# ScalarE in program order during the three attention sweeps of a pre-norm block

## The chip, the cores and the metric

The kernel runs on one core of a Trainium2 chip. A core has five engines that run side by side and wait for one another by semaphores: TensorE (PE in the profile, its weight loads PEld), VectorE (DVE), ScalarE (ACT), GpSimd (POOL) and SyncE (SP, which here only issues transfers). Each engine takes its instructions one after the other from its own list. The metric is the device time of one execution in microseconds; the time of the kernel before is the median of three runs.

## The reference

One transformer block with 2048 tokens of width 1024, in float32:

```
x = x + attn(layernorm(x))
x = x + ffn(layernorm(x))

attn: q, k, v = h @ w.T + b, each as 32 heads of 32
      scores[s] = q[s] k[s]^T / sqrt(32)       # 32 x 32, heads against heads, per token
      context[s] = softmax(scores[s]) v[s]
ffn:  dq(w) = NF4 quantise and dequantise, blocks of 64 with their own absolute maximum
      (silu(h dq(w1)^T) * (h dq(w2)^T)) dq(w3)^T        # width 2752
```

Attention is between the heads of one token, so it never mixes tokens. The weights of the feed-forward come unquantised: quantising and dequantising 2752 x 1024 numbers three times is part of the work.

## The kernel before

**Three sweeps.** Attention goes over the tokens three times: sweep 1 computes q for all of them, sweep 2 computes k, the scores and the softmax, sweep 3 computes v, the context, the residual and the second layernorm. A sweep has 8 pairs (`for p in range(NP)`), a pair being 256 tokens. In the trace sweep 1 runs from 13 us to 244 us, sweep 2 to 498 us, sweep 3 to 776 us; what follows is the feed-forward.

**One pair.** `products` multiplies by a scheme of seven products instead of eight; each is 8 matmuls on PE (3.43 us, L326). Four of them add up in one bank `z` (three in sweep 1, where the sixth product has a bank `y` of its own), two in a bank `q`, one stands in `r`. The partial sums are needed between the products, so ACT copies them out: `g0` after the first product, `s7` from `q` after the second, `u2` after the third, `u4` after the fifth, and (in sweeps 2 and 3) `ce` after the sixth. As `z` goes on adding, PE may not start the third product (`T2`) before `g0` is copied, the fifth (`T1`) not before `u2`, the sixth (`B22`) not before `u4`. Between the products stands a call `fill(n)` with n = 7, 6, 2, 5, 3, 4 in this order, where other work is put:

- sweep 1, `fill(5)`: 16 transposes of the next pair's tokens on PE (L458), each group of four copied out twice by ACT (L461, L462); three PSUM buffers.
- sweep 2, `fill(7)`, `(2)`, `(5)`, `(4)`: half of the small score matmuls of one tile each (`part`, L406). After a second half comes the softmax: DVE takes the maximum (L562) and subtracts (L564), ACT takes the exponential (`pr`, L570), DVE sums, divides and transposes.
- sweep 3: context matmuls instead (L420), after a second half the residual and a layernorm on DVE; in `fill(5)` and `fill(3)` transposes (`keep_T`, L680) that ACT copies (L681).

**The background.** A generator (`background`) quantises the feed-forward weights, one [128, 1024] block (a job) at a time, and `advance(n)` takes n steps of it. A job has 17 steps. Twelve of them are one ACT instruction (`sg`, L229) and one DVE instruction that takes it in (`r`, L230); three are DVE alone; one is the next job's `absmax`: a DVE maximum, two small DVE instructions and 16 ACT multiplies (L182, `wn`); the last is 16 ACT multiplies of the result (L182, `r`), the scale step. `sg` has two buffers, `r` has two, so an `sg` waits for the DVE instruction two before it. Sweep 1 takes 7 steps in each pair (six fills without the fifth, and two at the pair's end), sweep 2 takes 8, sweep 3 takes 9. When the scale step is through, `flush` issues the job's transposes on PE (`ptw`, L156), half a job at a time, with an ACT copy each (`wop`, L157): in sweep 1 ahead of the steps of `fill(7)` and `fill(3)` and after the pair's products, in sweep 2 after the steps of `fill(5)` and `fill(3)` and after the pair's products, in sweep 3 after those of `fill(7)` and `fill(4)` and after the products.

**Who sets the order.** PE executes in the order of the program from the first sweep on (`manual_schedule`, L270). The order on ACT, DVE and the queues is set at build time by the scheduler: it plays the program through and, whenever an engine is free, gives it that ready instruction which stands first in the program. So an instruction of the background that is ready may be put ahead of a copy that still waits. What the scheduler has put into ACT's list stays there: the rows of ACT in the trace follow one another in exactly that order.

Of the kernel before, what the change touches and what calls it, by code (L numbers as in the profile page):

```python
# [68 lines left out]
def preln_block_kernel(  # L69
# [14 lines left out]
    nc = tc.nc  # L84
# [182 lines left out]
    pair = left.enter_context(tc.tile_pool(name="pair", bufs=1, side="left"))  # L267
    ps_pj = left.enter_context(tc.tile_pool(name="ps_pj", bufs=1, space=PSUM, side="left"))
    small = right.enter_context(tc.tile_pool(name="small", bufs=2, side="right"))
    ctx.enter_context(tc.manual_schedule(engines={nc.tensor.engine}))  # L270

    NP = NT // 2
    SA11, SA12, SA22, S1, S2, S3, S4 = range(7)
# [425 lines left out]
    for p in range(NP):  # L699
# [36 lines left out]
        advance(2)  # L736
        A = nextA
    hook["scale"] = "DVE"
    left.close()


# [317 lines left out]
```

## Time and profile before

| what | value |
|---|---|
| time, median of 3 runs | 2529.96 us (2529.02 to 2530.29) |
| the profiled execution | 2526.8 us, its span 2525.0 us |
| mean granted TensorE clock in it | 0.991 |
| busy, share of the span | PE 97%, DVE 76%, ACT 62%, POOL 4% |
| sweep 1, 13 to 244.4 us | PE 215.23, DVE 221.47, ACT 129.31 us busy of 231.4 |
| sweep 2, 244.4 to 498.2 us | PE 248.56, DVE 212.42, ACT 120.52 us busy of 253.8 |
| sweep 3, 498.2 to 776.2 us | PE 260.55, DVE 240.60, ACT 129.36 us busy of 278.0 |

A row of the timeline has the start in us, how long the piece lasts, the engine, the line of the kernel, the operation, what it writes `<-` what it reads, the shape and the number of instructions merged into the piece; brackets hold the idle time of the engine ahead of it and who ended that. A row of the waits has the engine, the line and what waited `<-` the engine, the line and the operand that released it, then the total in us, how often, and the longest.

### The profile page before, as it was taken

To read this page: it belongs to the slowest core of one execution; us is meant where nothing else is said; L and a number is where in the kernel's file an instruction comes from. 1 tells how busy PE (TensorE), PEld (TensorE's weight loads), DVE (VectorE), ACT (ScalarE), POOL (GpSimd) and SP (SyncE) were. 2 spreads that over 40 slices of the span, in tenths; PEclk is the share of its full clock that TensorE was granted. 3 is DMA by queue.
4 is the path that set the end of the run, shared out by engine and by line. 5 is a ranking of instruction groups with operands and counts; after the bars stand their busy time and mean duration, and the time that the engine had idled before them with its cause. 6 is when DMAs were issued, how large, how long until landed. Compare 5 with 4: busy or idle time off the path is not lost.

```text
span 2525.0 us, 36235 instructions
## 1 busy us (share of the span) xinstructions
PE 2445.7 (97%) x14160; PEld 1146.6 (45%) x14160; DVE 1923.1 (76%) x2088; ACT 1564.9 (62%) x3147; POOL 104.9 (4%) x152
## 2 busy tenths in 40 slices
PE   8999999999998999999999999999999999999998
PEld 4444455544444444444444444444444444444433
DVE  8999788878898578978789788887878878851022
ACT  3556544344543478878788787888877888851100
POOL 1010000000000000010000100001000010000100
PEclk9999999999999999999999999999999999999999
DMA  8779633656678574453743547436375353641574
GB/s 306 298 287 358 234 142 129 240 193 214 222 231 298 171 229 113 146 142 134 241 121 136 135 145 238 129 112 159 126 227 151 116 146 126 226 133 63 109 287 141
DMA packets 145323, 464.04 MB, mean 184 GB/s; under 512 B 12352, under 2 KB 66624, under 8 KB 125312
## 3 DMA queue, kind: packets, MB, share of 16 engines
q1 hardware_dynamic: 133056, 419.73, 45.9%
q0 software_dynamic: 11520, 41.95, 9.9%
q8 instruction: 111, 1.82, 0.3%
q14 instruction: 60, 0.49, 0.1%
q10 hardware_dynamic: 576, 0.05, 0.0%
HBM read 275.82 MB, written 185.86 MB: 183 GB/s over the span
## 4 chain that ended last, share of the span: by engine, by line
DVE 29%; PE 25%; ACT 11%; issue 4%; DMA 1%; DVEq 0%; ACTq 0%
DVE r L230 21%; PE po L951 12%; PE z L326 7%; ACT wn L182 4%; ACT r L182 3%; PE q L326 3%; ACT sg L229 2%; DVE r L223 2%; DVE r L225 2%; PE rr L326 1%; DVE am L194 1%; DVE r L241 1%; ACT wop L157 1%; PE po L963 1%; PE ptw L156 0%
## 5 line engine op out<-in xcount | busy, mean ns | idle before, releaser
L229 ACT ACTIVATE sg<-wn 128x1024 f32<-128x1024 f32 x780 | 814.3, 1051 | 358.1 <-DVE r L230 351.5
L230 DVE SCALAR_TENSOR_TENSOR r<-sg,r 128x1024 f32<-128x1024 f32 x780 | 946.9, 1214 | 68.5 <-ACT sg L229 26.2
L951 PE MATMUL po<-w,h 128*128 128x512 f32 x1344 | 594.0, 596 | 6.6 <-ACT acc L975 3.2
L951 PEld LDWEIGHTS po<-w,h 128*128 128x128 f32 x1344 | 250.0, 190 | 324.2 <-issue 288.3
L326 PE MATMUL z<-xB,w 128*128 128x512 f32 x720 | 325.4, 600 | 3.5 <-ACT u L889 1.8
L326 PE MATMUL z<-xT,w 128*128 128x512 f32 x656 | 296.3, 594 | 5.2 <-ACT u L882 5.0
L326 PE MATMUL q<-xT,w 128*128 128x512 f32 x656 | 290.9, 592 | 0.0
L182 ACT ACTIVATE wn<-wn,rc 128x64 f32<-128x64 f32 x1032 | 262.2, 336 | 45.1 <-DVE rc L202 45.1
L326 PEld LDWEIGHTS z<-xB,w 128*128 128x128 f32 x720 | 134.6, 192 | 166.9 <-issue 151.7
L326 PEld LDWEIGHTS q<-xT,w 128*128 128x128 f32 x656 | 123.6, 190 | 151.4 <-issue 149.2
L326 PEld LDWEIGHTS z<-xT,w 128*128 128x128 f32 x656 | 121.9, 190 | 153.9 <-issue 138.2
L326 PE MATMUL q<-wT,A 128*128 128x512 f32 x384 | 174.5, 598 | 2.3 <-DVE A L385 2.3
L326 PE MATMUL z<-wT,A 128*128 128x512 f32 x384 | 175.5, 600 | 1.1 <-ACT u L345 0.8
L326 PE MATMUL z<-wB,A 128*128 128x512 f32 x320 | 152.0, 619 | 13.4 <-ACT u L345 13.4
L182 ACT ACTIVATE r<-r,am 128x64 f32<-128x64 f32 x608 | 153.8, 339 | 14.7 <-DVE r L230 14.7
L326 PE MATMUL rr<-xB,w 128*128 128x512 f32 x328 | 147.5, 592 | 0.0
L975 ACT COPY acc<-po 128x512 f32<-128x512 f32 x160 | 91.3, 571 | 73.0 <-PE po L951 71.3
L194 DVE TENSOR_REDUCE am<-wn 128x16 f32<-128x1024 f32 (+1 forms) x65 | 78.4, 1206 | 76.1 <-ACT r L182 70.0
L981 POOL DMA_DIRECT2D x1d<-acc x80 | 70.2, 877 | 1497.3 <-ACT acc L975 1497.3
L326 PEld LDWEIGHTS q<-wT,A 128*128 128x128 f32 x384 | 72.6, 192 | 90.4 <-issue 84.8
L326 PEld LDWEIGHTS z<-wT,A 128*128 128x128 f32 x384 | 70.3, 190 | 79.8 <-issue 76.7
L885 DVE TENSOR_TENSOR g<-g,rr 128x512 f32<-128x512 f32 x41 | 28.0, 682 | 102.4 <-PE rr L326 102.4
(112 smaller groups left out, 2100.5 us busy)
## 6 DMA issues: line engine op xcount, KB each, us to landing
w<-wd SPq DMA_DIRECT2D x41, 1280.0 KB, 6.9
wd<-wop SPq DMA_DIRECT2D x21, 2048.0 KB, 6.7
x1d<-acc POOLq DMA_DIRECT2D x80, 512.0 KB, 5.1
wn<-in_w_dram SPq DMA_DIRECT2D x63, 512.0 KB, 3.9
w<-wd SPq DMA_DIRECT2D x62, 512.0 KB, 4.1
xT<-xdT SPq DMA_DIRECT2D x28, 1024.0 KB, 7.7
xB<-xdB SPq DMA_DIRECT2D x24, 1024.0 KB, 5.5
opD<-A SPq DMA_DIRECT2D x8, 1792.0 KB, 5.9
```

The lines of the kernel that those rows point to most:

```text
L157: nc.scalar.copy(o[:q, first + half], pt[:q])
L182: nc.scalar.mul(dst[:, ts(n, BLOCK)], src[:, ts(n, BLOCK)], by[:, n : n + 1])
L194: nc.vector.tensor_reduce(am[:, :nb], v.rearrange("p (b e) -> p b e", e=BLOCK), AX.X, ALU.max, apply_absolute_value=True,)
L223: nc.vector.scalar_tensor_tensor(r, v, edge, r, ALU.is_lt, ALU.max)
L225: nc.vector.scalar_tensor_tensor(r, v, edge, r, ALU.is_gt, ALU.subtract)
L229: nc.scalar.activation(t, v, AF.Copy, bias=-edge * by, scale=by)
L230: nc.vector.scalar_tensor_tensor(r, t, code, r, ALU.min, ALU.max)
L326: nc.tensor.matmul(dst, w[:, k, :], xop[:, k, :], start=start and k == 0, stop=stop and k == 3, skip_group_check=True,)
L885: nc.vector.tensor_tensor(self.g0, self.g0, r, ALU.add)
L951: nc.tensor.matmul(po, hs[c][j][:, ts(q, P)], w3T[c][:, ts(n, 512)], start=(c == g[0]), stop=(c == g[-1]), skip_group_check=True,)
L975: nc.scalar.copy(a[:, ts(n, 512)], po)
L981: nc.gpsimd.dma_start(x1d[i], a, accum_op=ALU.add)
```

## The change

During the three sweeps ACT is put under `manual_schedule` too, beside PE: it gets its instructions in the order in which the program issues them. After the last pair of sweep 3 that context is closed and the one for PE alone opened again, so from the feed-forward on the scheduler orders ACT as before. No instruction is added, taken away or changed, and the text of the program keeps its order.

```diff
-    ctx.enter_context(tc.manual_schedule(engines={nc.tensor.engine}))
+    by_hand = ExitStack()
+    by_hand.enter_context(
+        tc.manual_schedule(engines={nc.tensor.engine, nc.scalar.engine})
+    )
...
         advance(2)
         A = nextA
     hook["scale"] = "DVE"
+    by_hand.close()
+    ctx.enter_context(tc.manual_schedule(engines={nc.tensor.engine}))
     left.close()
```

## The prediction

> **What bounds the kernel now.** I read the page first: PE is busy 97% of the span, so time is gained or lost where PE waits. The change touches the sweeps alone, so I asked for PE's waits between 13 and 776.2 us (columns: who `<-` whom, us in total, times, longest):
>
> ```profile
> PE z L326 <- ACT u L345: 14.2, 6, 4.3
> PE pt L458 <- ACT V L462: 12.5, 4, 4.3
> ...
> PE pt L458 <- ACT AV L462: 1.0, 3, 0.3
> ```
>
> 27.7 us of PE's idle time end on an ACT copy. That is all that a better order on ACT can give, with what the clock adds. Next the timelines of PE and of ACT at the longest wait of sweep 3:
>
> ```profile
> 618.62 1.09 PE L680 MATMUL pt<-ident,x 128*128 128x128 f32 x8
> 624.02 5.40 PE L326 MATMUL z<-wB,A 128*128 128x512 f32 x8 [4.30 <-ACT u L345]
> ```
>
> ```profile
> 619.78 1.06 ACT L229 ACTIVATE sg<-wn 128x1024 f32<-128x1024 f32 x1 [6.05 <-DVE r L230]
> 621.11 1.06 ACT L229 ACTIVATE sg<-wn 128x1024 f32<-128x1024 f32 x1 [0.27 <-DVE r L230]
> 622.43 1.06 ACT L229 ACTIVATE sg<-wn 128x1024 f32<-128x1024 f32 x1 [0.27 <-DVE r L230]
> 623.40 0.57 ACT L345 COPY u<-z 128x512 f32<-128x512 f32 x1
> ```
>
> The product before ended at 617.4. The copy `u4` of it, at 623.40, stands behind three `sg` that come later in the program and run in step with DVE. PE idles 4.30 us, and its next eight matmuls take 5.40 us where 3.70 is usual: the granted clock is halved for 3.4 us. Such slow pieces follow the five long waits (4.04, 4.31, 4.30, 3.31, 3.69) with 1.1, 2.2, 1.7, 1.5 and 2.8 us above 3.70, together 9.3.
>
> The other side: the background runs far ahead of its place. Count its steps (7 a pair in sweep 1, 8 in sweep 2; scale steps are numbers 17, 34, 51, 68, 85, ... from 0). Number 68 belongs to sweep 2, pair 1, `fill(3)`; its PE transposes follow at once. The 16 multiplies and those transposes (ACT, then PE):
>
> ```profile
> 245.79 2.98 ACT L182 ACTIVATE r<-r,am 128x64 f32<-128x64 f32 x12 [0.57 <-DVE r L230]
> 248.67 0.56 ACT L345 COPY g<-z 128x512 f32<-128x512 f32 x1
> 249.14 1.06 ACT L182 ACTIVATE r<-r,am 128x64 f32<-128x64 f32 x4
> ```
>
> ```profile
> 293.64 3.70 PE L326 MATMUL z<-wB,A 128*128 128x512 f32 x8
> 297.18 0.60 PE L156 MATMUL ptw<-ident,r 128*128 128x128 f32 x4
> 297.62 3.60 PE L326 MATMUL q<-wT,A 128*128 128x512 f32 x8
> ```
>
> They were done 47 us before PE asked. In the order of the program that lead is gone.
>
> **What goes.** With program order no later `sg` stands before a copy: all six `u` waits and the `pt` waits go, **-27.7 - 9.3 = -37.0 us**. What is late next is DVE in sweep 1: it is busy 221.47 of 231.4 us, some of it for steps ahead of their place, so part of sweep 1's 13.5 + 3.3 us may stay. That goes into the range.
>
> **What comes, where the place is known.** A block of 16 multiplies takes 3.84 us of ACT (33.24 to 37.08, below). In program order it can hold up PE in two ways: a copy queues behind it, or `ptw`, which PE meets right after the step, waits for it.
>
> (a) Sweep 1, pair 0, `fill(7)`: the first `absmax`. Its block started at 33.24, when its load and DVE were through; before it ACT copied `u2`:
>
> ```profile
> 28.38 0.59 ACT L345 COPY u<-z 128x512 f32<-128x512 f32 x1 [3.39 <-PE z L326]
> 33.24 3.93 ACT L182 ACTIVATE wn<-wn,rc 128x64 f32<-128x64 f32 x16 [4.27 <-DVE rc L202]
> 37.08 0.56 ACT L345 COPY u<-z 128x512 f32<-128x512 f32 x1
> ```
>
> Now `u2` comes after it, at 37.08, and `T1` starts at 37.65 in place of 31.61: +6.0 and, after such a gap, a slow piece (mean of the five: 1.9): **+7.9** (6 to 9).
>
> (b) Step 68: the block must follow `ce`, which ACT starts at 297.38 and leaves at 297.86; 3.84 us later, with 0.1 to pass it on, `ptw` starts at 301.8, not 297.18: +4.6, slow piece 1.9: **+6.5** (4.6 to 7.4).
>
> (c) Step 85, sweep 2, pair 3, `fill(4)`: the block (in this trace at 271) must follow this fill's exponential, and `ptw` comes right after the scores:
>
> ```profile
> 365.78 1.81 PE L406 MATMUL sc<-kd,ql 32*32 32x32 f32 x128
> ...
> 367.52 0.66 PE L156 MATMUL ptw<-ident,r 128*128 128x128 f32 x4
> ...
> 369.09 1.22 DVE L562 TENSOR_REDUCE mx<-sc 128x32 f32<-128x1024 f32 x1
> ...
> 370.34 1.23 DVE L564 TENSOR_TENSOR pr<-sc,mx 128x1024 f32<-128x1024 f32 x1
> ...
> 371.60 1.06 ACT L570 ACTIVATE pr<-pr 128x1024 f32<-128x1024 f32 x1 [2.80 <-DVE pr L564]
> ...
> 372.56 0.57 ACT L345 COPY g<-z 128x512 f32<-128x512 f32 x1
> ```
>
> ACT is free at 372.56, the block ends at 376.4, `ptw` starts at 376.5: +9.0, or 7.8 if DVE takes `mx` one instruction earlier; slow piece up to 2.8: **+11** (7.8 to 12).
>
> (d) Step 34, the last of sweep 1's pair 4: PE wants its `ptw` two products (6.9 us) later; the block follows a `DVE r` that stands behind the pair's adds and transposes, 3 to 10 us of DVE. Late by 0 to 7: **+4**.
>
> (e) Pair ends of sweep 2 with a block (steps 62, 79, 102, 119): from the end of the scores `mx` and the subtraction take 2.3 us, the exponential 1.0, two `sg` 1.9, the block 3.84, `g0` 0.5: 9.5; PE needs `g0` after two products and a half of scores, 8.6. Each 0.9 late, up to 2 where a scale step must first wait for its `r`: **+5** (0 to 8).
>
> (f) Step 153, sweep 3, pair 3, `fill(4)`: the block follows a DVE step beside the residual: **+2** (0 to 4). The other blocks fall where the next copy is due 8 us or more later: 0.
>
> Sum: **+36.4** (18 to 47).
>
> **What comes everywhere.** ACT now also waits, with all copies behind it, for DVE: `sg` for the `r` two before, the exponential for `mx` and the subtraction. At a pair's end in sweep 2 without a block the chain is 2.3 + 1.0 + 3 x 0.96 + 0.5 = 6.7 us against 8.6: cover for one late DVE instruction (1.13 us from start to start), not for three. With DVE busy 84% (sweep 2) to 96% (sweep 1) I take 0.6 us a pair (bounds 0 and 1.5, the third instruction): **+14** over 24 pairs (0 to 36).
>
> The lead lost is made good after the sweeps: DVE is busy 87.35 of the 123.8 us after 776.2, so 36 us are free against some 2 jobs of 17 steps at 1.13. I cost it at 0; if that cover failed, PE would wait for `ptw` there.
>
> In this trace an idle gap of 3.31 us (before 662.00) was followed by the slow clock, one of 2.86 us (before 212.17) was not. The page "TensorE: Matmul & The Clock Gate" of the Trainium skill, section "HAM oscillation", puts the limit a little higher, at idle gaps of about 3.4 us. By that rule the gap of 3.31 us would have brought no slow piece and the gain would be 1.5 us less; the row decides.
>
> **Sum.** -37.0 + 36.4 + 14 = +13.4. The profiled execution took 2526.8, which gives 2540.2; the median of the runs is 3.2 above it: **2543**.
>
> **Rivals.**
>
> 1. *Faster:* the 37.0 us go in full and the blocks cost only what no DVE order can help: (a) 6, (b) 4.6, (c) 7.8, nothing per pair: -18.6, **2511**. This needs DVE to run its steps where they stand: it decides for faster once named blocks and pairs together stay under 32 us. For it: PE has no ACT wait above 2.1 us in the whole of sweep 2, where DVE has 16% to spare. Against it: (a) to (c) follow from the order alone.
> 2. *Lockstep:* each pair costs its 1.5 us (36), the blocks 47, and sweep 1's 16.8 us aren't won since DVE is full: +63, **2593**. For it: sweep 1's DVE. Against it: the end of a pair has its 1.9 us of cover.
> 3. *No change* (within 0.2%, 5 us, about what a measurement of this kernel can tell): gain and cost meet. That the order stays as it is can't be the reason: the block of step 68 must move by 50 us.
>
> **Chances.** Forecast (2535 to 2570) 0.48, lockstep (above) 0.11, no change 0.14, faster 0.27. Below 2512 and above 2580 I leave some 0.07 each, so the range is 2512 to 2580. Faster 0.27, same 0.14, slower 0.59.
>
> **What would show it.** The rows `PE z <-ACT u` of 3 to 4 us in sweep 3 gone; sweep 3 shorter by 10 us or more, sweep 2 longer by 20 to 35, sweep 1 within 10. New waits of PE: `z L326 <- ACT u` of 6 us near 32 us, `ptw L156 <- ACT r L182` of 4 to 5 and 8 to 9 us in sweep 2, each with slow matmuls behind it. I am wrong if `ptw` doesn't wait (the blocks still run early), or if DVE is full in sweep 2, or if the feed-forward grows longer.

## The result, and the profile after

| | before | after |
|---|---|---|
| median of 4 runs each, us | 2530.12 (2529.02 to 2530.54) | 2551.98 (2549.35 to 2557.13) |
| ratio, 95% interval | | 1.009 (1.0072 to 1.0107) |
| profiled execution, span, us | 2526.8, 2525.0 | 2557.13, 2555.3 |
| mean granted TensorE clock | 0.991 | 0.984 |

The change makes the kernel 21.9 us slower; +13.4 was forecast. The profiled execution of after is the longest of its four, 5.2 us above their median, while that of before lies 3.3 us below its own, so the traces show a difference of 30.3 us. I follow those 30.3.

First PE's waits of after between 13 and 800 us, the view that opened the prediction:

```profile
PE ptw L156 <- ACT r L182: 10.6, 5, 6.5
PE z L329 <- ACT g L348: 10.6, 4, 3.7
PE z L329 <- ACT u L348: 6.6, 2, 5.9
PE sc L409 <- issue: 3.3, 3, 2.7
PE pt L461 <- ACT AV L465: 2.9, 7, 0.8
```

The row of 12.5 us for `pt` behind `V` is gone, and of the 14.2 us for `u` one new wait of 5.9 is nearly all that is left. In their place stand waits that before did not have: for the scale step's result (`ptw`) and for `g0`. Then the stages of after: sweep 1, 2, 3, the *tail* (from the first product behind sweep 3 to the first product of the feed-forward's second unit) and the units up to 1324.5. The columns are the stretch, its length, busy us (instructions) of PE, PEld, DVE, ACT and POOL, the granted clock, the DMA share and GB/s.

```profile
12.90:245.80 232.90, 218.08 (x587) 101.91 (x586) 209.49 (x283) 112.54 (x246) 13.92 (x28) 0.96 0.82 307
245.80:521.10 275.30, 258.79 (x4058) 135.07 (x4056) 207.22 (x210) 109.98 (x217) 0.00 (x0) 0.96 0.47 175
521.10:795.80 274.70, 261.81 (x4559) 137.71 (x4554) 241.67 (x255) 130.36 (x287) 22.05 (x26) 0.98 0.67 229
795.80:874.10 78.30, 62.28 (x778) 31.77 (x777) 64.41 (x71) 46.39 (x89) 4.60 (x6) 0.87 0.70 231
874.10:1324.50 450.40, 447.54 (x1138) 202.28 (x1137) 357.85 (x368) 350.57 (x696) 21.28 (x24) 1.00 0.52 159
```

The last two stretches as before had them:

```profile
776.20:844.10 67.90, 59.52 (x779) 30.61 (x778) 47.77 (x54) 25.58 (x44) 4.27 (x6) 0.92 0.79 262
844.10:1294.50 450.40, 447.53 (x1138) 202.13 (x1137) 357.81 (x368) 350.68 (x696) 21.31 (x24) 1.00 0.52 159
```

With before's sweeps of 231.4, 253.9 and 277.9 us the difference is +1.5, +21.4, -3.2, +10.4 in the tail, and nothing in the units after it. The tail is the surprise: ACT is the scheduler's again there, yet it grows by a sixth, with 71 DVE instructions instead of 54, and the clock falls to 0.87.

**The new wait of sweep 2.** PE, ACT and DVE of after, in the pair where sweep 2 loses most (32.20 to 46.42 us), at the second of its two waits:

```profile
376.16 1.78 PE L409 MATMUL sc<-kd,ql 32*32 32x32 f32 x128
384.47 1.91 PE L156 MATMUL ptw<-ident,r 128*128 128x128 f32 x4 [6.53 <-ACT r L182]
386.17 4.89 PE L329 MATMUL z<-wB,A 128*128 128x512 f32 x8
```

```profile
379.40 1.19 DVE L565 TENSOR_REDUCE mx<-sc 128x32 f32<-128x1024 f32 x1
380.51 1.20 DVE L394 TENSOR_TENSOR kd<-kd,kb 128x1024 f32<-128x1024 f32 x1
381.64 1.21 DVE L567 TENSOR_TENSOR pr<-sc,mx 128x1024 f32<-128x1024 f32 x1
```

```profile
382.89 1.06 ACT L573 ACTIVATE pr<-pr 128x1024 f32<-128x1024 f32 x1 [8.51 <-DVE pr L567]
383.85 3.91 ACT L182 ACTIVATE r<-r,am 128x64 f32<-128x64 f32 x16
```

ACT idles 8.51 us before the exponential, because the next thing in the program is that exponential and DVE has still to take the maximum, an add of its own, and subtract. Behind it stand the 16 multiplies; PE's transposes need them. But PE does not wait for the sixteenth: it starts at 384.47, 0.62 us into the block of 3.91. Each transpose reads 128 columns, which are two multiplies. The other kind of wait, at the end of the pair before, ACT then PE:

```profile
347.54 3.93 ACT L182 ACTIVATE wn<-wn,rc 128x64 f32<-128x64 f32 x16
351.36 0.58 ACT L348 COPY g<-z 128x512 f32<-128x512 f32 x1
```

```profile
352.00 6.69 PE L329 MATMUL z<-wT,A 128*128 128x512 f32 x8 [3.40 <-ACT g L348]
```

Here a copy stands behind the whole block; and the eight matmuls behind the wait take 6.69 us instead of 3.70.

**The tail.** PE, then DVE of after, at the longest wait of the whole trace:

```profile
836.61 3.60 PE L329 MATMUL z<-xB,w 128*128 128x512 f32 x8
848.86 1.94 PE L683 MATMUL pt<-ident,x 128*128 128x128 f32 x8 [8.65 <-DVE x L324]
850.60 4.79 PE L329 MATMUL z<-xB,w 128*128 128x512 f32 x8
```

```profile
842.42 1.22 DVE L230 SCALAR_TENSOR_TENSOR r<-sg,r 128x1024 f32<-128x1024 f32 x1
...
843.70 1.23 DVE L223 SCALAR_TENSOR_TENSOR r<-wn,r 128x1024 f32<-128x1024 f32 x1
...
845.43 1.23 DVE L225 SCALAR_TENSOR_TENSOR r<-wn,r 128x1024 f32<-128x1024 f32 x1
...
846.77 1.23 DVE L230 SCALAR_TENSOR_TENSOR r<-sg,r 128x1024 f32<-128x1024 f32 x1
847.91 0.81 DVE L324 TENSOR_SCALAR x<-x,mv,rs 128x1024 f32<-128x1024 f32 x1
```

PE has nothing to do until the last layernorm (L324) is written, and that one waits its turn among steps of the background. To see why there are so many of them here, I count the background's DVE rows (L230, 12 of a job's 17 steps) stage by stage, after and then before. The columns are the stretch, its length, busy us of these rows and their number, then clock, DMA share, GB/s.

```profile
12.00:245.80 233.80, 44.77 (x37) 0.96 0.82 308
245.80:521.10 275.30, 56.24 (x46) 0.96 0.47 175
521.10:795.80 274.70, 61.70 (x51) 0.98 0.67 229
795.80:874.10 78.30, 28.24 (x24) 0.87 0.70 231
```

```profile
12.00:244.40 232.40, 57.01 (x47) 0.97 0.83 312
244.40:498.30 253.90, 58.93 (x48) 1.00 0.50 188
498.30:776.20 277.90, 59.56 (x49) 0.98 0.67 227
776.20:844.10 67.90, 14.59 (x12) 0.92 0.79 262
```

At the end of sweep 1 the background has done 37 of these steps instead of 47, at the end of sweep 3 134 instead of 144; the tail then takes 24 instead of 12. Program order gives up a **lead** of about ten such steps, and the scheduler, let loose again, rebuilds it at once.

### The profile page after: what moved, and what is told of

The parts are those of the page before. It is cut to its first block, busy times and chain, and to the rows that moved or that the text cites. A ratio compares the mean times of both kernels' runs of the same rounds, so it can differ in the third digit from the quotient of the medians.

```text
span 2555.3 us, 36189 instructions
## 1 busy us (share of the span) xinstructions
PE 2462.8 (96%) x14160; PEld 1151.5 (45%) x14160; DVE 1923.7 (75%) x2088; ACT 1559.2 (61%) x3147; POOL 113.1 (4%) x152
## 4 chain that ended last, share of the span: by engine, by line
DVE 33%; PE 22%; ACT 11%; issue 5%; DMA 2%; DVEq 0%; POOL 0%; ACTq 0%
DVE r L230 22%; PE po L956 11%; PE z L329 6%; ACT wn L182 4%; ACT r L182 3%; PE q L329 3%; ACT sg L229 2%; DVE r L223 2%; DVE r L225 2%; DMA xdT<-xU 1%; PE rr L329 1%; DVE am L194 1%; DVE r L241 1%; ACT wop L157 1%; PE po L968 1%
## 5 line engine op out<-in xcount | busy, mean ns | idle before, releaser
L230 DVE SCALAR_TENSOR_TENSOR r<-sg,r 128x1024 f32<-128x1024 f32 x780 | 948.1, 1216 | 120.1 <-ACT sg L229 78.6
L329 PE MATMUL z<-xB,w 128*128 128x512 f32 x720 | 325.7, 600 | 3.4 <-ACT u L894 1.8
L329 PE MATMUL z<-xT,w 128*128 128x512 f32 x656 | 298.1, 597 | 8.8 <-ACT u L887 5.4
L329 PE MATMUL q<-xT,w 128*128 128x512 f32 x656 | 291.0, 592 | 0.0
L329 PEld LDWEIGHTS z<-xB,w 128*128 128x128 f32 x720 | 134.9, 192 | 167.0 <-issue 152.0
L329 PE MATMUL z<-wT,A 128*128 128x512 f32 x384 | 187.7, 634 | 16.8 <-ACT g L348 10.6
L329 PEld LDWEIGHTS z<-xT,w 128*128 128x128 f32 x656 | 122.5, 191 | 158.7 <-issue 138.6
L329 PEld LDWEIGHTS q<-xT,w 128*128 128x128 f32 x656 | 123.7, 190 | 151.4 <-issue 149.2
L329 PE MATMUL q<-wT,A 128*128 128x512 f32 x384 | 176.4, 603 | 3.5 <-DVE A L388 2.5
L329 PE MATMUL z<-wB,A 128*128 128x512 f32 x320 | 149.4, 611 | 0.7 <-ACT u L348 0.7
L329 PE MATMUL rr<-xB,w 128*128 128x512 f32 x328 | 147.5, 592 | 0.0
L329 PEld LDWEIGHTS z<-wT,A 128*128 128x128 f32 x384 | 74.7, 202 | 103.4 <-issue 84.1
L329 PEld LDWEIGHTS q<-wT,A 128*128 128x128 f32 x384 | 73.2, 193 | 92.9 <-issue 85.9
```

What stands on the lines that cost most here:

```text
L230: nc.vector.scalar_tensor_tensor(r, t, code, r, ALU.min, ALU.max)
L329: nc.tensor.matmul(dst, w[:, k, :], xop[:, k, :], start=start and k == 0, stop=stop and k == 3, skip_group_check=True,)
```

## The experiments

Theory: the loss has two causes, blocks that stand where the program puts them (in the sweeps), and the lost lead, which is paid for by the first stage that rebuilds it. Rivals: waiting for DVE in every pair (lockstep); block length alone; early steps in the tail as such. Stage lengths are in us, from one profiled execution each, and can differ by 0.1 from the rounded windows above. Their spread where the scheduler orders ACT in both: sweep 1 lasts 231.4 to 235.7 us in before, s3_only, s3_tail, s3_mid and s3_slow_start, sweep 2 253.2 to 253.9.

| run | median, us | before beside it | ratio (95%) | sweep 1 | sweep 2 | sweep 3 | tail | units to the 11th behind it |
|---|---|---|---|---|---|---|---|---|
| before | 2530.12 | | | 231.4 | 253.9 | 277.9 | 67.9 | 450.4 |
| after | 2551.98 | 2530.12 | 1.009 (1.0072-1.0107) | 232.9 | 275.3 | 274.7 | 78.4 | 450.4 |
| s1_only | 2540.23 | 2526.32 | 1.0061 (1.0045-1.0077) | 230.3 | 265.6 | 282.4 | 66.4 | 450.6 |
| s2_only | 2556.97 | 2526.32 | 1.0128 (1.0112-1.0144) | 232.7 | 273.4 | 287.8 | 66.6 | 450.3 |
| s3_only | 2526.61 | 2526.32 | 1.0 (0.9988-1.0012) | 235.7 | 253.5 | 268.8 | 77.7 | 450.4 |
| late_flush2 | 2544.77 | 2527.52 | 1.0062 (1.0048-1.0075) | 232.5 | 261.4 | 270.3 | 83.8 | 450.6 |
| one_mul | 2532.0 | 2527.52 | 1.0012 (1.0002-1.0022) | 225.8 | 259.9 | 268.1 | 84.6 | 450.3 |
| one_mul_sched | 2535.58 | 2530.01 | 1.0019 (1.001-1.0029) | 233.9 | 261.0 | 279.5 | 68.8 | 450.3 |
| hand_tail | 2555.18 | 2527.52 | 1.0106 (1.0091-1.0121) | 230.3 | 275.4 | 271.4 | 79.4 | 450.3 |
| s3_tail | 2530.71 | 2527.52 | 1.0014 (1.0005-1.0022) | 231.6 | 253.2 | 269.0 | 80.6 | 450.7 |
| hand_pass | 2552.97 | 2530.01 | 1.0089 (1.0075-1.0103) | 232.5 | 275.1 | 269.0 | 67.8 | 462.5 |
| s3_mid | 2531.47 | 2530.01 | 1.0008 (0.9999-1.0017) | 232.6 | 253.4 | 279.9 | 72.8 | 450.4 |
| s3_slow_start | 2519.05 | 2529.71 | 0.9957 (0.9944-0.997) | 233.1 | 253.5 | 268.2 | 67.3 | 456.9 |

**One sweep at a time.** The context for PE and ACT covers only one sweep; in the other two PE alone is held. In s1_only it is closed behind the loop of sweep 1; s2_only and s3_only enter it later:

```diff
-    by_hand.enter_context(
-        tc.manual_schedule(engines={nc.tensor.engine, nc.scalar.engine})
-    )
+    by_hand.enter_context(tc.manual_schedule(engines={nc.tensor.engine}))
...
+    by_hand.close()
+    by_hand.enter_context(
+        tc.manual_schedule(engines={nc.tensor.engine, nc.scalar.engine})
+    )
```

> ACT in program order in sweep 1 alone. Block theory (PE waits where a block of 16 ACT multiplies stands right before something that PE needs, because the background has lost its lead; the scheduler rebuilds the lead as soon as it orders ACT again): sweep 1 within 3 us of before, and from sweep 2 on everything as before, 2527 to 2535 us. Rival, a lead that is lost costs later whenever it is lost (DVE has the same work left and no spare time): 2538 us or more.

> ACT in program order in sweep 2 alone. Block theory: the waits of sweep 2 (+21 us between the first products of sweep 2 and of sweep 3 in the changed kernel) all come back, sweep 3 goes as in the kernel before, with its three waits on u4, and the tail after sweep 3 too: 2547 to 2555 us. Rival (the cost of the change is spread over all that follows, or sits at the borders where the context is closed): less than 2542 us, with the difference somewhere else.

> ACT in program order in sweep 3 alone. Block theory with a tail that pays for the lost lead: sweep 3 some 3 to 8 us shorter than before, the 70 us after it some 10 us longer, 2530 to 2540 us. Rival (the tail's loss in the changed kernel came from what sweeps 1 and 2 left undone): the tail as before and sweep 3 shorter, below 2528 us.

Of the times, that of s1_only lies in the rival's range, that of s2_only above both, that of s3_only in the rival's range, though its tail grew as the theory said. The counts of L230, as above, for sweep 2 of s1_only, sweep 3 of s2_only, then sweep 2 and the tail of s3_only:

```profile
243.00:508.70 265.70, 71.24 (x59) 0.97 0.49 183
```

```profile
519.00:806.60 287.60, 75.50 (x62) 0.95 0.65 221
```

```profile
248.20:501.80 253.60, 45.24 (x37) 1.00 0.51 190
...
770.50:848.20 77.70, 28.35 (x24) 0.87 0.71 233
```

Sweep 1 alone: sweep 1 itself comes out level (230.3), but sweep 2, which the scheduler orders, is 11.7 us longer, 10.1 of it in its first two pairs (26.41 and 32.50 us become 28.46 and 40.53). It does 59 of these steps instead of 48, after 37 instead of 47 in sweep 1. Sweep 2 alone: +19.5 in sweep 2, and +9.9 in sweep 3, where 62 steps are done instead of 49. Sweep 3 alone: -9.1 in sweep 3, +9.8 in the tail, where 24 are done instead of 12; the median does not move. So each sweep also costs something outside itself, in the stage that follows the program's order, and nearly the same sum.

Three things limit this reading. In s3_only the lead is gone at the end of sweep 2 already (37 instead of 48), where the scheduler still orders ACT, and sweep 2 is no shorter for it (253.5). In s2_only the first pair of sweep 3 is 6.9 us longer, but PE waits for neither ACT nor DVE in it: it idles 4.3 us in `issue`, with slow matmuls behind; the second pair, 3.7 us longer, has a wait of 4.0 us for DVE. And sweep 3 of s1_only is 4.5 us longer as well, at the usual 49 steps: PE's waits are no longer than in before, the granted clock is 0.95 instead of 0.98. The counts and lengths show where the debt is paid; how steps turn into waiting is seen row by row only in the tail.

**The transposes later.** `flush` in the sweeps waits until the next job is some steps old, so that the block is done when PE gets there. The first attempt, late_flush, took `range(3, 15)`:

```diff
+    def flush_late():
+        if step.get("n") in range(3, 14):
+            flush(1)
...
-                flush(1)
+                flush_late()
```

> The changed kernel, with the PE transposes of a job issued only from the third step of the next job on instead of right after its scale step, in all three sweeps. Block theory: the waits of PE for the scale step (1.2 + 6.5 us in sweep 2, 2.0 in sweep 3, 0.7 in sweep 1) and the slow clock behind them (1.7 + 4.5 + 3.4 us) go, the waits on g0 at pair ends stay: 2532 to 2540 us. Rival (DVE or ACT is what is late, PE's place of waiting only shows it): the waits move to the next copy and the time stays above 2546 us.

> The changed kernel with the PE transposes of a job issued only in steps 3 to 13 of the next job, so that at least four steps of the background stand between a scale step and the PE transposes that read it (the first try let them through while the step number was still 14). Block theory: PE has no wait of over 1 us on the scale step any more (6.5 us in sweep 2's pair 3, 2.0 us in sweep 3), sweep 2's pair 3 falls from 46 us to 36 us or less, the waits on g0 stay; in all 14 to 18 us under the changed kernel's 2552, so 2533 to 2540 us. Rival (the wait only shows at the transposes, ACT is late for the next copy in any case): the pair keeps 42 us or more, with the wait on g0 or u2 instead, and the time stays above 2546 us.

late_flush did not do what was meant: right behind the scale step the step number still is 14, so the transposes that mattered stayed where they were (2558.17 against 2526.32, 1.0134, 1.0119 to 1.0149), and the pair of the trace above kept a `ptw` wait of 6.46 us. late_flush2, with 14, does it. PE's waits of late_flush2 between 13 and 777 us (four lines were added, so L333 and L352 are L329 and L348 of after):

```profile
PE z L333 <- ACT g L352: 15.9, 5, 4.4
PE z L333 <- ACT u L352: 6.1, 2, 5.9
```

No `ptw` is left, and that pair takes 34.31 us instead of 46.42; sweep 2 is 13.9 us shorter than in after. The waits for `g0` stay, and grow by 5.3 us. The tail is longer still, 83.8: the part of the loss that lies there isn't touched. So the median is only 7.2 us below that of after, where 14 to 18 were expected.

**Short blocks.** Both blocks of a job are cut to one multiply until the end of the sweeps, so that 15 of 16 are left out, with program order (one_mul) and, as a control, with the scheduler (one_mul_sched):

```diff
-        for n in range(nb):
+        for n in range(nb if hook["scale"] == "DVE" else 1):
```

> The changed kernel with 1 of the 16 ACT multiplies of each absmax and each scale step until the end of the sweeps; 15 of 16 blocks of 64 columns are left unscaled, so this part of the computation is changed. Block theory: each block takes 0.3 us of ACT in place of 3.9, the named waits shrink by 3 to 4 us each and lose most of their slow clock; sweep 1 and 2 together fall by 20 us or more, 2522 to 2532 us. Rival (lockstep: it is DVE and the order that are late, not the blocks): less than 10 us gained, above 2540 us.

> The kernel before (ACT by the scheduler) with 1 of the 16 ACT multiplies of each absmax and each scale step until the end of the sweeps; 15 of 16 blocks of 64 columns are left unscaled, so this part of the computation is changed. It is the control for the changed kernel with the same edit. Block theory: with its lead the scheduled kernel hides the blocks, so it stays within 6 us of before, 2521 to 2530 us, and the gain of one_mul belongs to program order. Rival (fewer ACT instructions help either order alike): 2515 us or less.

PE's waits of one_mul between 13 and 767 us:

```profile
PE ptw L156 <- ACT r L182: 8.7, 4, 6.2
PE pt L461 <- ACT AV L465: 6.9, 7, 4.8
...
PE z L329 <- ACT u L348: 3.0, 2, 2.3
...
PE z L329 <- ACT g L348: 0.5, 1, 0.5
```

It is the mirror image: the waits for `g0` fall from 10.6 to 0.5 us and those for `u` are halved, but the `ptw` of 6.53 us still waits 6.23. So the `g0` waits come from the block's length, as does 3.6 of the 5.9 us of the `u` wait of (a), and the `ptw` waits come from what stands ahead of the block, the exponential with its two DVE instructions. The pair of (a) is hardly shorter even so (40.38 us, in after 40.76): a wait of 4.79 us for an `AV` copy comes instead, and that copy itself waits 4.35 us for the transfer `opV<-AV`.

In the same three sweeps one_mul takes 753.8 us and its control 774.4: with short blocks program order wins 20.6 us in the sweeps, of which the tail takes back 15.8. By the medians, each against its own before, the two are level (1.0012 and 1.0019). The 20.6 us are not all a gain of program order: the control's sweeps are 11.2 us longer than before's, though ACT has less to do (its traced execution lies 4.6 us above its median). 5.5 of the 7.1 us that its sweep 2 loses lie in the second pair, where PE waits for a transfer:

```profile
283.73 1.78 PE L406 MATMUL sc<-kd,ql 32*32 32x32 f32 x128 [3.93 <-DMA ql<-qD]
```

Why that transfer comes later there is open. Against before itself (763.2 in the three sweeps) one_mul wins 9.4 us.

**Holding ACT beyond the sweeps.** hand_tail closes the context behind the tail, s3_tail does the same on s3_only, hand_pass holds it until the first pass of the feed-forward is through:

```diff
-    by_hand.close()
-    ctx.enter_context(tc.manual_schedule(engines={nc.tensor.engine}))
...
         down(g, tbp, hs)
+        if by_hand is not None:
+            by_hand.close()
+            ctx.enter_context(tc.manual_schedule(engines={nc.tensor.engine}))
+            by_hand = None
         hs = {}
```

> The changed kernel with ACT kept in program order until the tail after sweep 3 (the last two tiles' context, residual and transposes beside the first plain block of the feed-forward) is through. Theory for the tail: there the scheduler takes background steps of later program places, which feed DVE and stand in its list ahead of the last residuals; with ACT held to the program those steps can't come early: the stretch from the first product after sweep 3 to the first seven-product unit falls from 98 us to 88 us and the time by 8 to 12 us, 2540 to 2544 us. Rival (the tail pays for work that sweeps 1 to 3 left undone and that must be done before the feed-forward starts): the stretch stays, or PE waits for weights in the units after it; 2550 us or more.

> ACT in program order in sweep 3 and its tail, by the scheduler before and after. Theory: sweep 3 wins its 9 us as with sweep 3 alone, and the tail doesn't give them back: 2515 to 2521 us beside some 2526 us of before on this chip. Rival (the tail pays for what is undone): 2526 us as with sweep 3 alone.

> The changed kernel with ACT kept in program order until the first pass of the feed-forward is through (its first down projection). In the kernel that closed the context after the tail, background steps of the first units still came ahead of the tail's copies, as they were outside the context; here they are inside. Theory 1 (early steps of later units fill DVE's list in the tail): the tail from the first product after sweep 3 to the first unit's sixth product falls from 78 to 70 us or less. Theory 2 (the lead has to be made up before the units need it): the tail may fall, but the units after it wait for scale steps by as much, and the time stays at 2548 to 2558 us. Theory 1 gives 2540 to 2546 us.

hand_tail and s3_tail miss their forecasts (2555.18 and 2530.71) and say little on the tail: steps that the program issues behind the close don't belong to the context, and the scheduler put them early all the same (an `sg` of the first unit at 806.77; 23 and 24 rows of L230 in the tail). hand_pass says more. Its tail and the stretch behind it, counted as above:

```profile
788.90:856.70 67.80, 12.93 (x11) 0.92 0.78 256
856.70:1319.20 462.50, 250.81 (x206) 1.00 0.52 157
```

With 11 rows the tail is as short as before's. But 206 instead of 192 follow, and the stretch behind is 12.1 us longer. PE's waits of hand_pass from 860 to 1000 us show it waiting there, where before and after have no wait in the same part of the units:

```profile
PE z L329 <- ACT u L885: 5.6, 2, 4.6
PE z L329 <- ACT u L892: 3.0, 1, 3.0
```

Its time, 2552.97, lies in the range of theory 2. Taken out of the tail, the steps cost about the same in the first units, which speaks against the theory that being early in the tail is the loss. It does not settle it: 3.0, 0.9 and 1.1 us of waits lie in the held pass, where the blocks of 16 multiplies stand in program order too, and the longest, 4.63 us at 995.28, behind its down projection, where the scheduler orders ACT again.

**Giving the lead back inside sweep 3, or not at all.** s3_mid is s3_only with the context closed before the last two pairs of sweep 3. s3_slow_start is s3_only with hand_pass's close; in the feed-forward the program takes steps in proportion to the time of PE's work, and its first pass here takes 15% fewer:

```diff
-        owed += us * RATE
+        owed += us * (0.57 if by_hand is not None else 0.67)
```

> ACT in program order in the first six pairs of sweep 3, by the scheduler otherwise. If a lead must be made up after every stretch in program order, pairs 6 and 7 of sweep 3 pay for it with waits on u4 as in the kernel before, and the tail is as before (68 us): the gain of pairs 3 and 4 stays, 2518 to 2524 us beside 2527. Rival (the tail pays whatever happens two pairs earlier): tail 76 us or more and 2526 us or above.

> ACT by the scheduler in sweeps 1 and 2, in program order from sweep 3 until the first pass of the feed-forward is through, and in that pass the background advances by 0.57 steps per microsecond of matmuls in place of 0.67 (some 15 steps fewer, less than one job). Theory: a lead given up costs PE only because the steps fall due before DVE and ACT have the time; with fewer steps due in the first pass sweep 3 keeps its 9 us, the tail stays at 68 us as with the context held through the first pass, and the first units lose 0 to 6 us in place of 12: 2518 to 2525 us beside some 2527 of before. Rival (the first units pay for the blocks of 16 multiplies in program order, not for the number of steps): they lose 10 us or more and the time is 2527 to 2533 us.

s3_mid: the last two pairs take 39.96 and 38.42 us instead of 38.05 and 33.15, and the tail 72.8; nothing is won. s3_slow_start is faster than before and after, by 10.7 us against before. Its tail and the stretch behind it, counted as above:

```profile
767.20:834.50 67.30, 10.96 (x10) 0.92 0.78 254
834.50:1291.40 456.90, 239.99 (x197) 0.99 0.53 159
```

Sweep 3 keeps its 9.7 us, the tail stays short, and of the 14 steps that hand_pass made good behind the tail only 5 are; that stretch costs 6.5 us instead of 12.1. So fewer steps cost less, and the rival's 10 us or more did not come; but PE's one long wait there, 5.0 us at 969.88, is for a scale step's block. A kernel with the lower rate and the scheduler throughout was not run, so how much of the 10.7 us the rate would bring by itself stays open.

## Why the prediction was right, and where it wasn't

The sign, the range and the forecast's own interval held, and so did the core of the mechanism: the `u` waits go, waits for named blocks come. The terms below are measured in the two traced executions, which lie 30.3 us apart:

- **The gain, -37.0.** The long waits named went, with the slow matmuls behind them. Of the 27.7 us, 0.7 stay as a `u` wait in sweep 2 (263.80) and 2.9 as waits for `AV`, so 24.1 went. The sign "sweep 3 shorter by 10 us or more" did not come: its pairs 1 to 6 fell from 209.84 to 197.54 us, but pair 0 (+4.6, a block) and pair 7 (+4.5) gave most of that back, and 3.2 are left. In hand_pass, with the same order on ACT in the sweeps, pair 7 is 3.1 us shorter and the sweep 269.0; in s3_only the sweep wins 9.1.
- **(a), (b), (c), (d), (f)** were forecast at 31.4. Measured: (a) a wait of 5.91 and matmuls of 6.70 instead of 3.70, 8.9 against 7.9; (b) the pair grew by 4.2 against 6.5; (c) a wait of 6.53, transposes of 1.91 instead of 0.66 and matmuls of 4.89 instead of 3.70, 9.0 against 11; (d) the pair grew by 6.9 against 4; (f) 4.3 against 2 (the pair won 1.7 instead of the 6.0 of its old wait). Together 33.3. In (b) and (c) I let PE wait for the whole block; it waits for the first columns, some 3.3 us less.
- **(e)** was forecast at 5, at most 8. Measured about 16.7: the pair ends of steps 79 (3.40 and 2.99 of slow matmuls), 102 (its pair +5.7) and 119 (its pair +4.6). I took 2.3 us from the end of the scores to the end of the subtraction; at step 79 it is 4.7 (the scores end at 339.83, the exponential starts at 344.56), because DVE does a transpose and an add of its own in between. I also left out the slow matmuls behind each such wait.
- **Lockstep, +14.** It did not happen: the pairs of sweep 2 that neither a long wait of before nor one of (a) to (f) touches take 32.31, 31.71 and 31.73 us, before 32.46, 33.11 and 32.69. The chain at the pair's end still fits, though with less margin than the 1.9 us I counted: in the pair of 31.71 us `g0` is copied at 427.47, 0.75 us before PE's next product (428.22). The chain of DVE and exponential costs PE something only where a block stands behind it.
- **The step that failed** is "The lead lost is made good after the sweeps ... I cost it at 0". It cost 10.4 us. The debt was not larger than I had counted (2 jobs have 24 L230 steps; the tail took 12 more than before), the cover was what failed: I counted DVE's free time over 123.8 us as if any of it would do, but the scheduler pays at once, in the stretch where the last layernorms bind PE. From 795.8 to 848.8 DVE is busy 51.18 of 53.0 us. The cover was named as one that could fail, with a wait for `ptw`; what came was a wait for DVE's layernorm. By its own sign, "I am wrong if ... the feed-forward grows longer", the prediction was wrong here.

With these values the sum is -37.0 + 33.3 + 16.7 + 10.4 = +23.4; the 3.6 us of waits that stayed and the 4.5 of pair 7 bring it to +31.5, beside the 30.3 of the traces. That +13.4 came so near the +21.9 of the medians is partly luck: +14 for nothing made up for much of what was missing, 11.7 in (e) and 10.4 in the tail.

Causes shown: what the `ptw` waits cost, by late_flush2; that the `g0` waits come from the block's length, by one_mul against its control; where the debt falls, by the counts and lengths of s1_only, s2_only and s3_only, and the tail's wait by DVE's rows. Argued only: that the steps as such, and not the blocks of 16 multiplies among them, make up the price of the debt in the first units, and why DVE, not ACT, sets it.

## What to carry to other kernels

A scheduler's early steps are a stock: ask how many units of background an order has in hand at each boundary, count them in the trace, and charge the difference to the stage that will rebuild it, at that stage's own bound. To put an engine in program order, first look at what long block stands before a copy that the critical engine needs, and what slow chain stands before the block; moving the consumer back (late_flush2) and cutting the block (one_mul) cure different waits. Total idle time of an engine was no cover here; idle time ahead of the binding instruction would have been.

## What the runs showed of the hardware

Short waits can bring the slow clock. In after, PE at step 68 (forecast (b)):

```profile
293.56 3.70 PE L329 MATMUL z<-wB,A 128*128 128x512 f32 x8
298.42 1.28 PE L156 MATMUL ptw<-ident,r 128*128 128x128 f32 x3 [1.16 <-ACT r L182]
```

After this wait of 1.16 us, and transposes in pieces, the granted clock is halved from 300.0 for 3.4 us; after one of 2.04 us (656.82) from 658.4 for 6.8 us, and the eight matmuls behind it take 5.99 us. The prediction weighed the page "TensorE: Matmul & The Clock Gate", section "HAM oscillation", of the Trainium skill, which puts the limit at idle gaps of about 3.4 us: in these two places no idle gap of PE was longer than 1.16 and 2.04 us, and the measurement decides. Nor does the length of a gap alone decide: the one of 2.86 us before 212.17 in before brought no slow clock, one of 2.83 us before the same transposes in s3_only (213.02) brought it from 212.2 for 6.8 us.

PE also stops for no wait that the profile shows: before seven score matmuls at 532.55 it idles 2.66 us, put down to `issue`, in the middle of one run of 128. In the same run of 128 hand_pass idles 2.85 us and before 2.01 (509.10). In after a wait of 1.45 us for `g0` follows it, and the clock is halved from 532.1 for 6.8 us.
